# The attention's values of sixteen heads in one unbroken run of matmuls, with six rooms for their operand in a weight slab's place

## The chip, the cores and the metric

The kernel runs on one core of a Trainium2 chip. The metric is the device time of one execution in microseconds (us), the median of several. The core's engines are PE (TensorE: matmuls, and the loads of their stationary operand), DVE (VectorE), ACT (ScalarE), POOL (GpSimd) and SP (SyncE, which here only issues DMAs). Each takes its own instructions strictly in the order of its queue and waits on semaphores for the others. SBUF is the working memory, 128 partitions wide; a size "of SBUF" here is always bytes in each partition. PSUM receives what PE computes.

## The reference

A decoder layer on `x` of 2 x 2048 x 512 and a context of 2 x 77 x 512, in float32: a state-space mixer, then cross attention to the 77 context rows, then a slot-based mixture of 16 experts, each followed by a residual and a LayerNorm. The change touches only the cross attention:

```python
q = (x @ q_w + q_b).reshape(B, T, H, D).transpose(0, 2, 1, 3)      # H = 16 heads of D = 32
k = (context @ k_w + k_b).reshape(B, S, H, D).transpose(0, 2, 1, 3)
v = (context @ v_w + v_b).reshape(B, S, H, D).transpose(0, 2, 1, 3)
att = jnp.einsum('bhtd,bhsd->bhts', q, k) / jnp.sqrt(jnp.float32(D))
att = jax.nn.softmax(jnp.where(causal[None, None, :, :], att, -jnp.inf), axis=-1)
y = jnp.einsum('bhts,bhsd->bhtd', att, v)
return y.transpose(0, 2, 1, 3).reshape(B, T, C) @ o_w + o_b
```

The line that the change rearranges is `y`: 16 products a row block, one for each head, of 77 context rows by 32 features.

## The kernel before

The kernel has four stages on one core. The mixer's scan runs to about 315 us. Then the attention stage goes over 16 tiles of 256 rows (`n` from 0 to 15, `N` = 16), each in two halves `s` of 128 rows; it also holds the mixer's output projection and LayerNorm ahead of the attention, and the dispatch to the slots behind it. Then the sixteen experts stream 192 weight slabs of 1 MB each, and a tail spreads the slots' result back over all rows.

In the attention stage each half tile passes through functions that the code calls by name:

- `load`, `scaled`, `out_proj`, `x1_transposed`, `queries`: the way to the queries, in hi/lo pairs (each product is three matmuls).
- `weigh(n, s, hg)`: scores and softmax of the four heads of group `hg` (0 to 3). DVE, ACT and POOL leave the probabilities in `pp`.
- `gather(n, s, hg)`: four transposes on PE (line 857) turn `pp`, and ACT (groups 0, 1 and 3) or DVE (group 2) copies the result from PSUM to the tile `pt`, 77 partitions by 512 numbers, 2,048 bytes. The pool gives `pt` three rooms (line 854).
- `values(n, s, hg)`: four matmuls, one for each head `r` of the group, with 32 columns of `vt` as the stationary operand. Head `r` writes partitions 32r to 32r + 31 of the PSUM tile `y`, of which there is one. They are in plain float32, and the profile shows two MATMUL records for each, so a group is eight records. After group 3, `y_halves` splits `y` into a hi and a lo tile (ACT, then DVE).
- `o_proj` and the rest: output projection, LayerNorm, the store of `x2` and, from `x2`, the slots' scores and sums (`dispatch`, `p_transposed`, `collect`).

The order of the calls is written out. `PLAN` has eight slots to a tile; in it "W", "G" and "V" stand for `weigh`, `gather` and `values` of the group that is due, with `values` two slots behind `weigh` and `gather` one behind. The lists `head` and `drain` give the first and last calls, and `last` those of the end, where tile 15's work stands in a fixed order on PE. All this sets priorities: the framework then lays out each engine's queue along a modelled timeline, in which an instruction is issued once its operands and its room are ready in the model, those traced earlier first. Two instructions can be tied in order without a wait (`tc.issue_after`, `add_manual_dep`).

The memory matters too. SBUF is two stacks. On the right stand the pools of the attention stage, each below the one that was opened before it: `b_in`, `b_zt`, `b_x1`, `b_sb` (16,736 bytes: maxima, sums, `pp`, the three rooms of `pt`, the halves of `y`), and lowest `b_sb2` (26,880 bytes: the rows `x2`, their halves, `x2T`, the slots' probabilities), which ends at byte 48,960. On the left, above constants and slot sums, stand the slabs A, B, C, ... of 8,192 bytes each for the experts' weights, from byte 15,488 on, over the same bytes that the attention uses from the other side. A slab whose bytes are free can be loaded while the attention runs; the others wait for their rooms. A to D end at 23,680, 31,872, 40,064 and 48,256; E to J follow to 97,408, and the slabs 0 to 9 lie under the right-hand weights. The order in which slabs are filled is written out as well:

```python
'first': 'ABCD06745981I3JK2GHFELM'   # e_Wg of expert 0 in A, B, C, D; its e_W1 in 0, 6, 7, 4; e_W2 in 5, 9, 8, 1; expert 1 from I on
```

Between 6 and 7 come the slots' own weights `d_Wv` and `d_Wo`, in L and M. All slabs are loaded by the SP queue (line 1228).

Of the kernel before, what the change touches and what calls it, by code (L numbers as in the profile page):

```python
# [1 line left out]

# [6 lines left out]
FP = mybir.dt.float32  # L9
# [7 lines left out]
S = 77  # L17
# [220 lines left out]
def tile_decoder(ctx, tc, a, out, dbg=None, upto=9, opt=None):  # L238
    nc = tc.nc
    dbg = dbg or {}  # L240
    opt = opt or TUNED
    pe, act, dve, pool = nc.tensor, nc.scalar, nc.vector, nc.gpsimd

    def mm(o, l, r, start, stop, **kw):
        return pe.matmul(o, lhsT=l, rhs=r, start=start, stop=stop, **kw)  # L245

    def cp(e, o, i):
        (act.copy, dve.tensor_copy, pool.tensor_copy)[e](o, i)  # L248
# [47 lines left out]
    vt = [kv_[b].tile([S, D], FP, name=f"vt{b}") for b in range(B)]  # L296
# [10 lines left out]
    with ExitStack() as st:  # L307
        class Pools:
# [8 lines left out]
            def tile(self, shape, dt, name, tag=None, bufs=1):  # L317
                return self.of[tag or name].tile(shape, dt, tag=tag or name, bufs=bufs, name=name)

        sb = Pools("a_sb", ("xt xh xl raw t1 hi lo dec e0", "BcE CE XE", "XO", "BcO", "CO",  # L320
                            "wtok wdt one chalf offs halo ut xw ssb Bt gm BS CS sw ctxT kst vb qs"), side="right")
# [331 lines left out]
        def chain(*fs):  # L653
            for f in fs:
                yield from f

        def next_weights():

            for j, nm, tags in ((1, "W_outT", ("hi", "lo")), (0, "q_w", ("xh", "xh")), (2, "o_w", ("xl", "xl"))):
                hi, lo = state[nm] = hi_lo_weights("w3", j)  # L660
                for k, tag in zip((0, 2), tags):
                    wr = sb.tile([128, 2, D], FP, tag=tag, bufs=1 + (j != 1), name="wr3")
                    nc.sync.dma_start(wr, rows_of(nm)[:, k:k + 2, :])
                    split(hi[:, k:k + 2], lo[:, k:k + 2], wr, engs[EA.get("wl%d" % j, 2 if j != 1 else 1)], EA.get("wh%d" % j, 0))
                yield
# [18 lines left out]
        for i in range(1, NT - 1):  # L684
            emit(SEQ.get("s%d" % i) or SEQ.get("s") or spread(("S", 16), ("P", 12), ("U", 3), ("V", 2)), "SP",
                 S=chain(scan(2 * i - 1), scan(2 * i)), P=project(i + 1), **later)
        emit(SEQ.get("l") or spread(("S", 16), ("W", 3)) + "S" * 8, "SWUV",
             S=chain(scan(2 * NT - 3), scan(2 * NT - 2), scan(2 * NT - 1)), W=next_weights(), **later)
# [41 lines left out]
    with ExitStack() as st:  # L730
        psb = {tag: st.enter_context(tc.tile_pool(name="b_" + tag, bufs=n, space=PSUM, reuse_waits="tile"))
               for tag, n in (("y", 1), ("mm", 2), ("tr", 2), ("sc", 2))}
        sbq, sb1, sb0 = (st.enter_context(tc.tile_pool(name=nm, bufs=1, side="right", reuse_waits="tile"))
                         for nm in ("b_q", "b_x1T", "b_in"))
        sbz, sbx, sb = (st.enter_context(tc.tile_pool(name=nm, bufs=1, side="right", reuse_waits="tile"))
                        for nm in ("b_zt", "b_x1", "b_sb"))
        sb2 = st.enter_context(tc.tile_pool(name="b_sb2", bufs=1, side="right", reuse_waits="tile"))

        def PT(tag, shape=(128, 512), bufs=2):
            return psb[tag].tile(list(shape), FP, tag=tag, bufs=bufs, name=tag)  # L740
# [14 lines left out]
        N = B * NT  # L755
        ts = [dict() for _ in range(N)]
# [94 lines left out]

        def gather(n, s, hg):
            pp = ts[n].pop(("pp", s, hg))
            pt = sb.tile([S, 4, 128], FP, tag="pt", bufs=opt.get("pt", 3), name="pt")
            tp = PT("tr")
            for r in range(4):
                pe.transpose(tp[0:S, r * 128:r * 128 + 128], pp[:, r, :], ident)  # L857
            cp(EN.get('g%d' % hg, 1 - hg % 2), pt, tp[0:S, :].rearrange("p (r t) -> p r t", t=128))
            ts[n]["pt", s, hg] = pt

        def values(n, s, hg):
            b = n // NT
            if hg == 0:
                ts[n]["y", s] = PT("y", bufs=1)
            yp = ts[n]["y", s]
            pt = ts[n].pop(("pt", s, hg))
            for r in range(4):
                h = hg * 4 + r
                mm(yp[32 * r:32 * r + 32, hg * 128:hg * 128 + 128], vt[b][:, 32 * h:32 * h + 32], pt[:, r, :], True, True)
            if hg == 3 and n < N - 1:  # L870
                y_halves(n, s)

        def y_halves(n, s):
            yh, yl = ts[n]["yv", s] = hi_lo("yv", [128, 4, 128], 1)
            yv = ts[n].pop(("y", s)).rearrange("p (k t) -> p k t", t=128)
            w = 2 if (n, s) == (N - 1, 1) else 4
            for k in range(0, 4, w):
                split(yh[:, k:k + w], yl[:, k:k + w], yv[:, k:k + w])
# [198 lines left out]
        def copy_turned(b, m):  # L1077
# [5 lines left out]
        LV, LG = opt.get("lv", 2), opt.get("lg", 1)  # L1083
        fns = {f.__name__: f for f in (load, scaled, x2_transposed, queries, dispatch, o_proj, p_transposed, out_proj, x1_transposed,
                                       collect, weigh, values, gather, y_halves, o_part, norm, normed, store, halves, x2_high, x2_low,
                                       scores, most, exponentials, sums_so_far, turned_high, turned_low, sums, add_sums, scale, turn_sums,
                                       copy_turned)}
# [103 lines left out]
    sb = cst_.enter_context(tc.tile_pool(name="c_sb", bufs=1, side="left", reuse_waits="tile"))  # L1191
# [3 lines left out]
    if True:  # L1195
# [18 lines left out]
        order, kept = first, {12 * (NE - NL): "0", 12 * NE + 1: "1", 12 * NE + 2: "2"}  # L1214
        while len(order) < 12 * NE + 3:
            n, free = len(order), "6745018923"
# [32 lines left out]
        for q in range(2):  # L1249
            aop = ps.tile([128, 2, B, 64], FP, tag=("mm", "w")[q], bufs=(2, 1)[q], name="aop")  # L1250
            for h in range(2):
                hg = 2 * q + h
# [59 lines left out]
    if True:  # L1312
# [165 lines left out]
        n = said = 0  # L1478
# [77 lines left out]
    with ExitStack() as st:  # L1556
        sb = st.enter_context(tc.tile_pool(name="f_sb", bufs=1, side="right", reuse_waits="tile"))
# [34 lines left out]
        live, at = {}, {}  # L1592
# [196 lines left out]
```

## Time and profile before

| what | value |
|---|---|
| median of three runs | 1490.38 us (1486.42 to 1490.95) |
| the profiled execution | 1492.08 us, its span 1490.2 us |
| mean granted clock of TensorE in it | 0.959 |
| PE busy over the span | 1357.0 us (91%) |
| DVE, ACT, POOL busy | 920.8, 623.2, 451.4 us |
| first and last `y` matmul | 349.8 and 894.9 us |
| first matmul of the experts | 933.4 us |
| last load of a weight slab lands | about 1398 us |
| slab D issued, slab I issued | 330.15 and 899.23 us |

The span is the time from the first to the last instruction; the execution has about 1.9 us around it. The strip in the profile cuts the span into 40 slices of 37.3 us, and each digit is the busy share in tenths. In the PE timeline, matmuls overlap: the next one starts before the modelled end of the one before, so what an instruction costs is the distance between starts. In a line of the timeline, `x8` means eight records in a row. In the list of waits the three numbers are the microseconds in all, the number of times and the longest.

### The profile page before, as it was taken

To read this page: it belongs to the slowest core of one execution; us is meant where nothing else is said; L and a number is where in the kernel's file an instruction comes from. 1 tells how busy PE (TensorE), PEld (TensorE's weight loads), DVE (VectorE), ACT (ScalarE), POOL (GpSimd) and SP (SyncE) were. 2 spreads that over 40 slices of the span, in tenths; PEclk is the share of its full clock that TensorE was granted. 3 is DMA by queue.
4 is the path that set the end of the run, shared out by engine and by line. 5 is a ranking of instruction groups with operands and counts; after the bars stand their busy time and mean duration, and the time that the engine had idled before them with its cause. 6 is when DMAs were issued, how large, how long until landed. Compare 5 with 4: busy or idle time off the path is not lost. (4 is left out here: it accounts for less than half of the span.)

```text
span 1490.2 us, 27755 instructions
## 1 busy us (share of the span) xinstructions
PE 1357.0 (91%) x10442; PEld 985.3 (66%) x10442; DVE 920.8 (62%) x2167; ACT 623.2 (42%) x1694; POOL 451.4 (30%) x498
## 2 busy tenths in 40 slices
PE   7899999978999999999999997978798989988796
PEld 6888878857888888888888786234354444432364
DVE  7997897857888888888888765011111111144397
ACT  5534544525665655665666563110000110034256
POOL 4634543535444444445443321000000000000045
PEclk9999999988999999999999999999998999999899
DMA  9889988894212212322210337999999999999547
GB/s 317 218 189 238 234 211 203 242 260 124 58 58 69 67 58 59 96 59 60 58 44 22 128 136 283 387 417 417 420 418 419 418 419 418 421 420 420 226 157 253
DMA packets 188062, 339.65 MB, mean 228 GB/s; under 512 B 12347, under 2 KB 135739, under 8 KB 163096
## 3 DMA queue, kind: packets, MB, share of 16 engines
q1 hardware_dynamic: 171632, 311.25, 60.3%
q10 hardware_dynamic: 16296, 26.62, 5.2%
q8 instruction: 83, 1.36, 0.4%
q14 instruction: 51, 0.42, 0.1%
HBM read 299.56 MB, written 38.27 MB: 227 GB/s over the span
## 5 line engine op out<-in xcount | busy, mean ns | idle before, releaser
L849 POOL TENSOR_TENSOR pp<-pp,den 128x308 f32<-128x308 f32 x128 | 89.8, 706 | 169.5 <-DVE den L848 65.6
L245 PE MATMUL up<-ew,hT 128*32 128x512 f32 x944 | 125.6, 614 | 10.4 <-DMA ew<-in_e_Wg 7.7
L1354 POOL MEMSET aT<- 128x512 f32 x16 | 8.3, 524 | 385.0 <-PE yac L245 385.0
L1413 DVE TENSOR_TENSOR Qc<-mm,vec 128x512 f32<-128x512 f32 x32 | 22.1, 691 | 149.8 <-PE mm L245 145.5
L245 PEld LDWEIGHTS mm<-xTh,cqh 128*128 128x128 f32 x256 | 50.4, 197 | 70.7 <-issue 42.7
L245 PE MATMUL mm<-xTh,cqh 128*128 128x256 f32 x256 | 81.0, 316 | 14.1 <-ACT xTh L248 14.1
L245 PE MATMUL yac<-ew,aT 128*32 128x512 f32 x488 | 72.7, 692 | 17.3 <-DMA ew<-in_e_W 10.6
L1345 ACT ACTIVATE sv<-up 128x512 f32<-128x512 f32 x32 | 19.1, 598 | 163.5 <-PE up L245 136.9
L248 ACT CAST xTh<-tr 128x512 fp32r<-128x512 f32 x32 | 18.7, 585 | 160.2 <-PE tr L1367 132.6
L857 PE MATMUL tr<-cst,pp 128*77 128x128 f32 x512 | 81.4, 283 | 2.7 <-DVE x1Tl L753 2.2
L248 ACT COPY pt<-tr 77x512 f32<-77x512 f32 x96 | 55.7, 582 | 61.5 <-PE tr L857 33.1
L245 PE MATMUL mm<-x1Th,w30h 128*128 128x256 f32 x256 | 76.4, 299 | 5.1 <-ACT x1Th L752 2.7
L847 ACT ACTIVATE pp<-sc,mx 128x77 f32<-128x77 f32 x240 | 75.3, 326 | 10.7 <-DVE mx L844 10.5
L245 PE MATMUL mm<-xTl,cqh 128*128 128x256 f32 x256 | 75.7, 296 | 2.9 <-DVE xTl L256 2.4
L245 PE MATMUL mm<-x1Tl,w30h 128*128 128x256 f32 x256 | 74.5, 291 | 0.5 <-DVE x1Tl L753 0.5
L245 PE MATMUL mm<-xTh,cql 128*128 128x256 f32 x256 | 74.3, 290 | 0.0
L245 PE MATMUL mm<-x1Th,w30l 128*128 128x256 f32 x256 | 73.9, 289 | 0.0
L857 PEld LDWEIGHTS tr<-cst,pp 128*77 128x77 f32 x512 | 60.1, 149 | 17.8 <-issue 11.4
L256 DVE TENSOR_TENSOR xTl<-tr,xTh 128x512 fp32r<-128x512 f32 x32 | 22.1, 691 | 77.8 <-ACT xTh L248 77.8
L544 DVE SCALAR_TENSOR_TENSOR X<-raw,vec,X 128x256 f32<-128x256 f32 x80 | 66.3, 874 | 5.4 <-ACT X L540 4.9
L775 POOL TENSOR_TENSOR ut<-ut,fb 128x512 f32<-128x512 f32 x32 | 41.4, 1298 | 72.1 <-DMA ut<-Ud 42.1
L248 ACT COPY raw<-pj 128x512 f32<-128x512 f32 x48 | 27.9, 583 | 75.0 <-PE pj L245 49.2
(387 smaller groups left out, 4348.6 us busy)
## 6 DMA issues: line engine op xcount, KB each, us to landing
ew<-in_e_W SPq DMA_DIRECT2D x122, 1024.0 KB, 16.2
ew<-in_e_Wg SPq DMA_DIRECT2D x57, 1024.0 KB, 16.2
BS<-scrBc SPq DMA_DIRECT2D x48, 256.0 KB, 5.1
CS<-scrC SPq DMA_DIRECT2D x48, 256.0 KB, 6.7
xs<-in_xT SPq DMA_DIRECT2D x32, 256.0 KB, 5.6
xt<-in_x SPq DMA_DIRECT2D x32, 256.0 KB, 2.8
ut<-Ud SPq DMA_DIRECT2D x32, 256.0 KB, 3.4
fb<-fd SPq DMA_DIRECT2D x128, 64.0 KB, 3.1
```

Source lines behind the costliest of these rows:

```text
L245: return pe.matmul(o, lhsT=l, rhs=r, start=start, stop=stop, **kw)
L248: (act.copy, dve.tensor_copy, pool.tensor_copy)[e](o, i)
L256: (lo_eng or dve).tensor_tensor(lo, src, hi, ALU.subtract)
L544: dve.scalar_tensor_tensor(dst, raw[:, j, 1 + t:1 + t + TB], w4[:, t:t + 1], dst, ALU.mult, ALU.add)
L775: (act, dve, pool)[EN.get('uf', 1)].tensor_tensor(ut, ut, fb, ALU.mult)
L847: act.activation(pp[:, r, :], sv[:, r, :], AF.Exp, bias=mx[:, h:h + 1], accum_out=den[:, h:h + 1])
L849: (act, dve, pool)[EN.get('d%d' % hg, 2)].tensor_tensor(pp, pp, den[:, h4].unsqueeze(2).to_broadcast([128, 4, S]), ALU.mult)
L857: pe.transpose(tp[0:S, r * 128:r * 128 + 128], pp[:, r, :], ident)
L1345: last["silu"] = act.activation(sv, up, AF.Silu)
L1354: pool.memset(aT, 0.0)
L1413: dve.tensor_tensor(Qc[b][:, mp * 2:mp * 2 + 2, t1:t1 + TB], qq, vec[:, V_CQ + mp * 2:V_CQ + mp * 2 + 2].unsqueeze(2).to_broadcast([128, 2 ...
```

## The change

For tiles 0 to 14, `values` of groups 0, 1 and 2 now does nothing. At group 3 it issues the products of all sixteen heads, group 3 first and then 0, 1 and 2, each matmul tied behind the one before it on PE, and then `y_halves`. Tile 15 keeps its four calls. So `pt` of the first three groups lives until the fourth is there; it gets six rooms instead of three, and a pool of its own, `b_pt`, opened last and so lowest on the right-hand stack. `b_sb` loses the three rooms (6,144 bytes), so that `b_sb2` moves up by as much, and `b_pt` (12,288 bytes) takes bytes 42,816 to 55,104. Slab D ends at 48,256.

```diff
-        sb2 = st.enter_context(tc.tile_pool(name="b_sb2", bufs=1, side="right", reuse_waits="tile"))
+        sb2, sbp = (st.enter_context(tc.tile_pool(name=nm, bufs=1, side="right", reuse_waits="tile")) for nm in ("b_sb2", "b_pt"))
...
-            pt = sb.tile([S, 4, 128], FP, tag="pt", bufs=opt.get("pt", 3), name="pt")
+            pt = sbp.tile([S, 4, 128], FP, tag="pt", bufs=opt.get("pt", 6), name="pt")
...
         def values(n, s, hg):
+
             b = n // NT
-            if hg == 0:
+            one_run = n < N - 1
+            if one_run and hg < 3:
+                return
+            if one_run or hg == 0:
                 ts[n]["y", s] = PT("y", bufs=1)
             yp = ts[n]["y", s]
-            pt = ts[n].pop(("pt", s, hg))
-            for r in range(4):
-                h = hg * 4 + r
-                mm(yp[32 * r:32 * r + 32, hg * 128:hg * 128 + 128], vt[b][:, 32 * h:32 * h + 32], pt[:, r, :], True, True)
-            if hg == 3 and n < N - 1:
+            at = None
+            for g in (3, 0, 1, 2) if one_run else (hg,):
+                pt = ts[n].pop(("pt", s, g))
+                for r in range(4):
+                    h = g * 4 + r
+                    order = tc.issue_after(at.ins) if at is not None else nullcontext()
+                    with order:
+                        at = mm(yp[32 * r:32 * r + 32, g * 128:g * 128 + 128], vt[b][:, 32 * h:32 * h + 32], pt[:, r, :], True, True)
+            if one_run:
                 y_halves(n, s)
```

More of the change, by code (lines that the diff above doesn't have):

```diff
@@ L1 @@
-from contextlib import ExitStack
+from contextlib import ExitStack, nullcontext
 import numpy as np
```

## The prediction

> **What bounds the kernel now.** I read the strip of forty slices first, then the busy times of four stretches that I cut at its breaks, then who waits for whom on PE, then the timelines of PE and of the SP queue. The strip:
>
> ```profile
> PE   7899999978999999999999997978798989988796
> DMA  9889988894212212322210337999999999999547
> ```
>
> In slices 10 to 23 (some 350 to 900 us, the attention) PE is full and DMA is not; from slice 25 on DMA is full. The stretches (columns: length, busy us of PE, PE weight loads, DVE, ACT, POOL, granted clock, DMA share, GB/s):
>
> ```profile
> 405.00:895.00 490.00, 484.21 (x3734) 407.35 (x3732) 396.18 (x1055) 295.04 (x985) 204.04 (x211) 1.00 0.22 69
> 895.00:933.00 38.00, 28.19 (x171) 22.19 (x163) 20.78 (x65) 12.37 (x32) 4.12 (x6) 0.88 0.80 296
> 933.00:1393.00 460.00, 397.71 (x2900) 182.00 (x2904) 91.73 (x173) 70.31 (x112) 8.06 (x16) 0.94 1.01 416
> ```
>
> The attention is bound by PE: 484 of 490 us busy at full clock, and its largest waits there, together about 5.4 us, begin
>
> ```profile
> PE mm L245 <- DVE ql L817: 2.4, 4, 0.6
> PE tr L750 <- DVE dtl L1020: 0.8, 2, 0.4
> PE y L245 <- DVE pt L248: 0.5, 2, 0.3
> ```
>
> The experts (933 to 1393) are bound by the stream of weights at 416 GB/s. That stream can't run far ahead: most slabs lie in rooms that the attention gives up at its end. So what the attention gives, the stream's start and the kernel's end move by, one for one. The 38 us between are a chain of short steps and move as a whole.
>
> What a run of `y` matmuls (the values) costs PE (columns: start, duration, engine, line, what, count; a group of four heads is x8, as each product is two passes):
>
> ```profile
> 602.02 0.39 PE L245 MATMUL mm<-w31l,yyh 128*128 128x512 f32 x1
> 602.24 0.39 PE L245 MATMUL mm<-w31h,yyl 128*128 128x512 f32 x1
> 602.56 0.43 PE L245 MATMUL y<-pt,vt 77*32 77x128 f32 x8
> 602.92 0.66 PE L857 MATMUL tr<-cst,pp 128*77 128x128 f32 x4
> 603.34 0.36 PE L245 MATMUL mm<-x1Th,w30h 128*128 128x256 f32 x1
> ...
> 476.37 0.86 PE L245 MATMUL y<-pt,vt 77*32 77x128 f32 x24
> 477.16 0.39 PE L245 MATMUL mm<-x1Th,w30h 128*128 128x256 f32 x1
> 477.38 0.28 PE L245 MATMUL mm<-x1Tl,w30h 128*128 128x256 f32 x1
> 477.50 0.29 PE L245 MATMUL mm<-x1Th,w30l 128*128 128x256 f32 x1
> ```
>
> Read starts, not durations. A 512-column product normally gives way after 0.23 us (602.02 to 602.24), ahead of `y` after 0.32: 0.09 lost on entry. One group holds PE 0.36 (602.56 to 602.92). What follows is late by 0.06 (four transposes took 0.42; undisturbed ones at 608.63 took 0.36) or by 0.10 (477.16 to 477.38 against 0.12 after it). A run of three groups holds PE 0.79, so each further group in a run adds (0.79 - 0.36) / 2 = 0.215.
>
> **The change, part by part.**
>
> *Runs joined.* A lone group costs 0.09 + 0.36 + 0.06 to 0.10 = 0.51 to 0.55 us, a joined one 0.215. Each run that disappears saves 0.30 to 0.335, say 0.31. The PE timeline from 349 to 895 has 103 `y` runs: 83 of one group, ten of two, eight of three, one group cut in two. The last seven, from 882.04 on, are tile 15's, which keeps its order. The 96 others become 30, one for each half tile of tiles 0 to 14: 66 fewer x 0.31 = **20.5 us** (ends 19.8 and 22.1).
>
> *Runs cut again.* The planner may put a matmul that falls due inside a run. Before, one group of 128 was cut, each having three inner seams: 1 in 384. Thirty runs of 15 seams: 450 / 384 = 1.2 cuts x 0.31 = **+0.4 us**.
>
> *New waits on PE.* With PE 4% shorter the others have less cover. DVE goes from 396/490 (81%) to 396/470 (84%), ACT from 60 to 63%; neither becomes the bound. The order on every queue is fixed beforehand, though, so single waits lengthen. Bounds: none, or all the saving (20 us). I take the nearer row, PE's present 5.4 us of waits, and let half as much again appear: **+3 us**.
>
> *Group 3 first.* The run waits for the newest copy `pt` (ACT, 0.58 us), and behind its first matmul all of PE queues. On the page of before, PE waits 1.1 us in total for `pt` ahead of all 103 runs: there is other work between a group's transposes and its values. The plan puts the gather of group 3 just ahead of the values of group 3, as before, so the same cover serves. 0; if it is gone, rival two.
>
> *Values of groups 0 to 2 later.* Their `pt` are held up to three groups longer, in six rooms instead of three; a half tile holds four and two are left for the next. ACT waited 28.0 us in all for `y` to free a `pt` room (11 times); that mostly ends and is off the path. The two splits of `y` (ACT 0.59, DVE 0.68) start 0.65 us later after group 3; `o_proj` stands two plan slots on, some 8 us. 0.
>
> There a rule of the Trainium skill speaks against the change. ACT's split waits for `y` 23.2 us in 17 cases now, with no PE wait behind it, and the next run that needs the single `y` bank starts some 17 us on. The page TensorEngine Tiling (Array Packing), section Performance Considerations, says that tiling speeds up TensorE but not the emptying of PSUM, which may become the bottleneck. By that rule, as an estimate, each of 30 runs would put 1.27 us of splits on the path, +38 us; by the row, nothing. The sum goes by the row.
>
> *Rooms moved.* By the tile sizes in the code the right-hand stack ended at byte 48,960 and slab D at 48,256. Now `b_sb2` starts 6,144 higher and the six rooms take 42,816 to 55,104, so three of them lie in D. The SP queue of before:
>
> ```profile
> 330.15 0.33 SPq L1228 DMA_DIRECT2D ewD<-in_e_Wg  x1
> ...
> 895.20 0.33 SPq L1228 DMA_DIRECT2D ew<-in_e_W  x1
> 899.23 0.33 SPq L1228 DMA_DIRECT2D ewI<-in_e_W  x1
> ...
> 918.87 0.33 SPq L1228 DMA_DIRECT2D ewG<-in_e_Wg  x1
> 919.29 0.38 SPq L1228 DMA_DIRECT2D ewH<-in_e_Wg  x1
> 919.77 0.38 SPq L1228 DMA_DIRECT2D ewF<-in_e_Wg  x1
> 928.40 0.33 SPq L1228 DMA_DIRECT2D ewE<-in_e_W  x1
> ```
>
> D (1 MB, 2.5 us at 416 GB/s) loses its early load and waits for the last values, about 895. I now lies under the end of `dtl`, whose last product (`mm<-x2h,dtl`) is at 916, and moves from 899 to 916. F comes to lie under the stored `x2` and waits, as E does, for a store that is issued at 921.2. D takes I's place ahead of 3, J, K and 2, which queue behind it; G and H may start with I. The share of DMA by 5 us slices between 895 and 935 leaves 7.6 us idle (most at 910 to 920), so one slab more can vanish. Bounds: -1 us (with F away from the ring the store lands sooner, and E, L and M follow it) and +2.5 us (a whole slab in a full stream). I take **+1**. D's absence at 330, where DMA is full, can help the first loads by up to 2.5 us, but no PE wait there is on D: 0.
>
> *Sum.* -20.5 + 0.4 + 3 + 1 = -16.1 us. The profiled execution took 1492.08 (span 1490.2 and 1.9 around it), so 1476.0 for such a one; the median of the three runs shown is 1490.38, 1.7 lower, and by it 1474.3. I say **1475**. A difference under 0.3% (4.5 us) counts as no change throughout.
>
> **The rivals.**
>
> *One, the gain is handed back.* The other queues' chains, not PE, come to set the pace: two thirds of the 20.5 turn into waits, 1490 - 7 + 1 = 1484, between 1480 and 1490. For it: DVE at 84%, POOL's `pp` waiting on DVE and ACT for over 100 us now. Against: PE waits 5.4 us in 490.
>
> *Two, slower: each run's head waits.* If the planner has nothing to put between the transposes of group 3 and the run, PE stands through transpose, ACT's queue and the 0.58 us copy. At the start of the attention, with nothing else to do, that cost 0.47 us (y at 349.84) and more where ACT was busy; 1.0 for each of 30 runs gives +30 - 20.5 + 1 = +10.5: 1501. It decides from 0.65 us a run. Against: 1.1 us of such waits now.
>
> *Three, D blocks the SP queue.* SP keeps its order. If D is queued where 6, 7, L, M, 4, 5, 9 and 8 go (840 to 892), these eight MB wait until 895: 20 us of transfers into 7.6 us of idle ring, +12.4 - 16: 1486. Against: the queue goes by when rooms come free (slab 7 was issued ahead of L although the code loads it after).
>
> **How the numbers follow.** Likeliest 0.58 (own range 1467 to 1482); rival one 0.18; rival two 0.14; rival three 0.10. Faster: 0.57 + 0.10 of one + 0.03 of three = 0.70; slower: 0.13 of two + 0.04 of three = 0.17; same 0.13. The range 1466 to 1494 leaves out most of rival two and a little below: under 2 in 10.
>
> **What would show it.** Right: some 37 `y` runs, thirty of x32 holding PE about 1.0 us; the stretch from the first `y` to the last some 16 us shorter; D issued near 880 and `hT` ready near 917 instead of 933; the stream's end and the tail behind it unchanged in length. Wrong: PE idle ahead of x32 runs with `pt` as releaser (two), PE waits on DVE and POOL of over 10 us in the attention (one), a hole in the SP queue after 840 (three), or runs cut in many pieces.

## The result, and the profile after

The changed kernel takes 1502.93 us (median of 7 runs, 1499.03 to 1509.06) against 1490.97 us for the kernel before in the same comparison: a ratio of 1.008, 95% interval 1.0058 to 1.0103. It is slower by 0.8%, some 12 us. 1475 was forecast. The profiled execution shown here took 1507.12 us (span 1505.3), 4 us more than the median, and 2.4 us of that lie ahead of the attention (the load of `xt` at 302.5 us in before comes at 304.9), where nothing was changed; differences between the two profiles are read with that in mind.

The stretches of the changed kernel (columns: length, busy us of PE, PE weight loads, DVE, ACT, POOL, granted clock, DMA share, GB/s), cut at its own landmarks, the last `y` matmul at 909.3 and the first matmul of the experts at 948.25:

```profile
405.00:909.40 504.40, 486.00 (x3791) 420.31 (x3789) 396.96 (x1065) 300.34 (x998) 204.16 (x212) 1.00 0.22 67
909.40:948.00 38.60, 28.33 (x171) 22.22 (x163) 21.01 (x66) 12.51 (x32) 4.12 (x6) 0.88 0.83 306
948.00:1408.00 460.00, 398.37 (x2903) 182.50 (x2904) 91.77 (x172) 70.16 (x112) 8.07 (x16) 0.94 1.01 417
```

The attention is 14.4 us longer (490.0 before; up to 2.4 of it is the late start), the steps behind it are 38.6 us (38.0), and the experts stream at 417 GB/s for the same length. So what the change lost it lost in the attention, and stream and tail only moved with its end. The granted clock in each stretch is that of before.

In the attention the runs of `y` came out as meant, where they are whole. From the timelines of PE in the changed kernel (columns: start, duration, engine, line, what, count), a whole run and one that the planner cut:

```profile
436.54 1.08 PE L245 MATMUL y<-pt,vt 77*32 77x128 f32 x32
...
447.03 0.30 PE L245 MATMUL sc<-kbh,ql 128*128 128x308 f32 x1
447.26 1.06 PE L245 MATMUL y<-pt,vt 77*32 77x128 f32 x26
448.25 0.39 PE L245 MATMUL mm<-x1Th,w30h 128*128 128x256 f32 x1
448.47 0.28 PE L245 MATMUL mm<-x1Tl,w30h 128*128 128x256 f32 x1
...
449.67 0.28 PE L245 MATMUL mm<-x1Th,w30l 128*128 128x256 f32 x1
449.88 0.42 PE L245 MATMUL y<-pt,vt 77*32 77x128 f32 x6
450.23 0.50 PE L245 MATMUL mm<-w31h,yyh 128*128 128x512 f32 x1
450.56 0.39 PE L245 MATMUL mm<-w31l,yyh 128*128 128x512 f32 x1
```

PE has 52 runs of `y` where before had 103. Of the thirty that should be whole, 16 are; 14 are in two pieces or more (seven of 26 and 6 records), all of them second halves of a tile, mostly with the twelve query products of the next tile in the gap. What PE waited for between 340 and 930 us in the changed kernel (columns: us in all, times, longest), the four largest rows, all of them ahead of a transpose:

```profile
PE tr L942 <- DVE pt L248: 5.8, 6, 1.0
PE tr L750 <- DVE x L792: 3.1, 1, 3.1
PE tr L857 <- DVE x2Tl L949: 3.0, 3, 1.1
PE tr L750 <- DVE dtl L1028: 2.5, 6, 0.4
```

All rows of this view together are 18.0 us in before and 29.3 us here; in the attention alone, from 405 us to the last `y`, they are 5.7 and 17.8. The slab D, of which the prediction spoke, is issued at 909.42, the moment the values end.

```profile
909.42 0.33 SPq L1236 DMA_DIRECT2D ewD<-in_e_Wg  x1
909.84 4.57 SPq L1236 DMA_DIRECT2D ew<-in_e_W  x2
```

So two things stood to be explained: why 20 us that PE was to save did not come, and why another 12 us were lost.

### The profile page after: what moved, and what is told of

It reads as the page before. It is cut to its first block, busy times and chain, and to the rows that moved or that the text cites. A ratio compares the mean times of both kernels' runs of the same rounds, so it can differ in the third digit from the quotient of the medians.

```text
span 1505.3 us, 27760 instructions
## 1 busy us (share of the span) xinstructions
PE 1353.1 (90%) x10442; PEld 992.3 (66%) x10442; DVE 917.0 (61%) x2167; ACT 624.8 (42%) x1694; POOL 452.5 (30%) x498
## 5 line engine op out<-in xcount | busy, mean ns | idle before, releaser
L857 PE MATMUL tr<-cst,pp 128*77 128x128 f32 x512 | 77.1, 279 | 7.3 <-DVE x2Tl L949 3.0
```

## The experiments

Laying out the queues is the planner's work, and with the change it laid out every queue of the attention anew: up to the first gathers PE's list is that of before, from there on VectorE, ScalarE, GpSimd and PE all stand in another order. To part this from the joining itself, most kernels below tie the queues to a written order. The tie waits for nothing; it only fixes which instruction follows which. The order is a list of positions kept in the kernel, and the diffs show how this list is made from that of before (`t` is the half tile, `d` where its groups stand, `q` the groups in that order, `f` whether an instruction is not of the values; `keep` leaves the groups where they stood, `joined` puts all four where the last stood). The late groups, the halves and the pairs take the groups as they stood, with group 3 last; the other kernels that join all four begin with group 3, as the changed kernel does. In the traces of the kernels "in the old order" the instructions other than the values follow each other on all four engines exactly as in before. Neither before nor the changed kernel was run with nothing but its own order tied, so what the tie alone might cost is not shown; a comparison of two tied kernels does not need it.

Theories one to four were: *one*, the new order loses the time; *two*, the joined run itself does, whatever the order; *three*, the six rooms in a slab's place; *four*, two PSUM rooms for transposes are too few. *Five* and *six* came after the first four runs: *five*, values that come late cost what joining saves; *six*, VectorE is full and PE's savings can't show. Ratios are to the kernel before, with 95% intervals.

**The joined runs in the old order.**

```diff
-                        at = mm(yp[32 * r:32 * r + 32, g * 128:g * 128 + 128], vt[b][:, 32 * h:32 * h + 32], pt[:, r, :], True, True)
+                        at = mm(yp[32 * r:32 * r + 32, g * 128:g * 128 + 128], vt[b][:, 32 * h:32 * h + 32], pt[:, r, :], True, True); YS.setdefault(2 * n + s, []).append(at.ins.name)
...
+        keep_order(tc, ['PE', 'DVE', 'Activation', 'Pool'])
...
+            for i in these:
+                if prev is not None:
+                    tc.add_manual_dep(i, prev.name, mybir.DependencyInfo(
+                        mybir.DependencyClass.NoSync, mybir.DependencyReason.DATA), reason="order")
+                prev = i
```

> The changed kernel, complete, with the queues of TensorE, VectorE, ScalarE and GpSimd tied to the order that they have in the kernel before; each joined run of values stands on TensorE where the last of its four groups stood. SP's queue is left to the planner. Nothing of the computation is left out. Theory one (the change made the planner lay out every queue of the attention anew, and the new order makes TensorE wait at its transposes for rooms that VectorE empties late): those waits go back to the 18 us that the kernel before has between 340 us and the attention's end, few or no runs are cut, and the joined runs bring what the prediction counted, about 15 to 20 us: 1470 to 1476 us, under the kernel before. Theory two (the joined run itself starves VectorE or waits for its last room, whatever the order): 1485 to 1505 us. Theory three (the six rooms in a slab's place cost it): 1495 to 1505 us, like the changed kernel.

Measured: 1491.35 us, 1.0008 (0.9997 to 1.0019). The 12 us of the changed kernel are gone, as theory one said, but the gain of 15 to 20 us is not there: all thirty runs are whole, hold PE 1.01 us, and the kernel takes as long as before. Both theories have half of it. Where the saving went shows in who waits, in the same stretch (405 to 895) of the two kernels. First before:

```profile
ACT pt L248 <- PE tr L857: 30.4, 35, 2.3
ACT pt L248 <- PE y L245: 25.2, 9, 3.1
ACT yvh L248 <- PE y L245: 21.0, 15, 2.5
DVE yvl L256 <- ACT yvh L248: 8.4, 11, 2.4
```

and the joined runs in the old order:

```profile
ACT pt L248 <- PE tr L857: 47.9, 37, 3.0
ACT yvh L248 <- PE y L245: 25.5, 25, 2.9
DVE yvl L256 <- ACT yvh L248: 15.7, 14, 2.9
PE mm L245 <- DVE ql L817: 6.7, 8, 0.9
```

With six rooms ACT no longer waits 25.2 us for `y` to free a room, but it waits 17.5 us longer for the transposes, and DVE stands longer ahead of the split of `y` (8.4 to 15.7). PE's own rows go from 18.0 to 30.2 us (340 to 930); the query products' wait for `ql`, which the prediction showed as 2.4, is 6.7. One such place, in before:

```profile
534.80 0.43 PE L245 MATMUL y<-pt,vt 77*32 77x128 f32 x8
535.15 0.66 PE L857 MATMUL tr<-cst,pp 128*77 128x128 f32 x4
535.57 0.39 PE L245 MATMUL sc<-kbh,qh 128*128 128x308 f32 x1
535.80 0.30 PE L245 MATMUL sc<-kbl,qh 128*128 128x308 f32 x1
535.94 0.28 PE L245 MATMUL mm<-x1Th,w30h 128*128 128x256 f32 x1
```

and with the joined runs (the bracket gives PE's idle time and what ended it):

```profile
531.79 0.60 PE L857 MATMUL tr<-cst,pp 128*77 128x128 f32 x4
532.14 0.39 PE L245 MATMUL sc<-kbh,qh 128*128 128x308 f32 x1
532.37 0.30 PE L245 MATMUL sc<-kbl,qh 128*128 128x308 f32 x1
533.42 0.39 PE L245 MATMUL mm<-x1Th,w30h 128*128 128x256 f32 x1 [0.75 <-DVE ql L817]
```

Before, a group of values stands here (another at 531.56), and the query product goes on without a wait. Joined, both groups stand further on, PE is there sooner, and it waits for VectorE, which takes about as long as before: from the start of `x1Tl` to the end of `ql` 4.7 us, 4.9 before, with one pause of 0.17 us in each. As the other instructions have the same order in both kernels, the distances between their starts on PE can be compared one by one. In the attention, from 340 us on, those next to a run of values shrink by 17.1 us, and all the others grow by 15.2: ahead of query products 7.2, of the transposes of `x` 3.8, of scores 2.6.

**The six rooms alone.**

```diff
-        sb2 = st.enter_context(tc.tile_pool(name="b_sb2", bufs=1, side="right", reuse_waits="tile"))
+        sb2, sbp = (st.enter_context(tc.tile_pool(name=nm, bufs=1, side="right", reuse_waits="tile")) for nm in ("b_sb2", "b_pt"))
...
-            pt = sb.tile([S, 4, 128], FP, tag="pt", bufs=opt.get("pt", 3), name="pt")
+            pt = sbp.tile([S, 4, 128], FP, tag="pt", bufs=opt.get("pt", 6), name="pt")
```

> The kernel before with the six rooms in a pool of their own (and the slabs that move with them) and nothing else: groups of values come one by one as before. Theory one: the planner lays out the queues anew here too, so the time is that of another order, within some 15 us of 1490 us to either side, and where it differs the difference stands in TensorE's waits before transposes, not in the slab stream. Theory three (the rooms cost it): 1500 us or more, as the changed kernel. If neither the order nor the rooms matter: 1488 to 1493 us.

Measured: 1491.53 us, 1.0001 (0.9986 to 1.0016). Neither the rooms nor the slabs that moved cost anything beyond some 2 us either way, and theory three falls. The planner laid out all queues anew here too, without loss: a new order as such need not cost. But it is much nearer to that of before: on PE 296 instructions other than the values have another place in the queue, in the changed kernel 1,543.

**Three rooms for transposes,** in the changed kernel and, as its control, in the kernel before.

```diff
-                for tag, n in (("y", 1), ("mm", 2), ("tr", 2), ("sc", 2))}
+                for tag, n in (("y", 1), ("mm", 2), ("tr", 3), ("sc", 2))}
...
-            return psb[tag].tile(list(shape), FP, tag=tag, bufs=bufs, name=tag)
+            return psb[tag].tile(list(shape), FP, tag=tag, bufs=3 if tag == "tr" else bufs, name=tag)
```

> The changed kernel with three rooms for transposes in PSUM where it has two (the attention uses seven of the eight banks). Theory four (two rooms for transposes are too few once the values come in one run): the waits before transposes, 23 us of the new ones, go, and the time is 1480 to 1488 us. Theory one (what counts is the order that the planner finds, and VectorE's lateness): part of the waits go from the transposes to the next room in the chain, and the time is anywhere from 1485 to 1510 us, another order again.

> The kernel before with three rooms for transposes in PSUM: the control of the run with three rooms. Theory four: the kernel before waits little for these rooms (tens of waits of 0.4 to 1 us, 18 us in all between 340 us and the attention's end), so at most 5 us are gained: 1485 to 1491 us. Theory one: another order, 1480 to 1505 us, and where it is slower the loss stands in TensorE's waits again.

Measured: 1496.77 us, 1.0045 (1.003 to 1.0061), and 1500.21 us, 1.0062 (1.0041 to 1.0083). With a third room the kernel before gets slower by 9 us. Both have yet another order (the first still has 14 of 30 runs in pieces, the control 112 runs of `y` instead of 103), so the two don't price the room by itself. They show that this room is no remedy, and how much a kernel in which nothing is joined can lose by a room and the order that comes with it. For theory four they are inconclusive. (Its 23 us of new waits were too many: the listed waits before transposes are 8.6 us in before and 21.9 in the changed kernel.)

**Late, but not joined.** In the old order, each of groups 0 to 2 ahead of one of the three instructions before group 3:

```diff
+def late(t, d, f):
+    if t >= 30: return keep(t, d, f)
+    q = list(d); spots = []; k = d[q[3]][0] - 1
+    while len(spots) < 3:
+        k -= 1
+        if f(k): spots.append(k)
+    spots = spots[::-1]
+    return [(spots[i], [q[i]]) for i in range(3)] + [(d[q[3]][-1], [q[3]])]
```

> The computation of the kernel before, with every queue in its order but for the values: groups 0 to 2 of a half stand late, each ahead of one of the three instructions that come before group 3, so that they are late but still four short runs with three breaks. Six rooms as in the changed kernel. Theory five (the values of a half that come late cost what joining saves: in the old place they were work for TensorE while VectorE and ScalarE were busy with the softmax; late, TensorE waits there and does them where the others wait for it): 12 to 17 us above the kernel before, 1502 to 1509 us; then joining brings about 15 us and moving costs about 15. Theory six (VectorE is simply full, whatever TensorE does): no change, 1488 to 1494 us.

Measured: 1519.02 us, 1.018 (1.0161 to 1.0198): 27 us slower. The edit does what it says (timeline of PE in this kernel):

```profile
549.33 0.28 PE L245 MATMUL mm<-x2Th,kql 128*128 128x256 f32 x1
549.54 0.43 PE L245 MATMUL y<-pt,vt 77*32 77x128 f32 x8
549.89 0.38 PE L245 MATMUL mm<-x2Th,kqh 128*128 128x256 f32 x1
550.21 0.42 PE L245 MATMUL y<-pt,vt 77*32 77x128 f32 x8
550.56 0.38 PE L245 MATMUL mm<-x2Tl,kqh 128*128 128x256 f32 x1
```

and these are its waits in the stretch of the two lists above:

```profile
ACT pt L248 <- PE tr L857: 48.5, 35, 3.0
ACT yvh L248 <- PE y L245: 42.7, 22, 3.9
DVE yvl L256 <- ACT yvh L248: 24.5, 13, 3.9
```

This is the sum that the prediction lacked. PE has 115 runs here, 12 more than before; at 0.31 us they are 3.7 of the 27 us, so lateness costs some 23. From here to the joined runs in the old order 78 runs go, at 0.31 some 24 us, and the two kernels differ by 1.72%, 25.6 us (22 to 29). So joining pays what was reckoned, and being late costs as much. ACT stands 42.7 us ahead of the split of `y` where it stood 21.0, with everything queued behind it. Start by start on PE, the distances away from the values grow by 18.5 us over before, much as with the joined runs (15.2); those next to the values grow by 9.7, more than the 3.7 reckoned for 12 runs. So 15 to 18 us of the price stand at the other instructions, and the rest lies at the short runs themselves. Theory six falls as it was put: VectorE has the same work, and the time moves by 27 us.

**One half at a time,** in the old order (the run of a half where its last group stood, the other half as before):

```diff
-place = joined
+place = lambda t, d, f: (joined, keep)[t % 2](t, d, f)
```

and with `(keep, joined)` for the other half.

> Every queue in the order of the kernel before; the values of each tile's first half (s = 0, tiles 0 to 14) come in one run where the last of their groups stood, those of the second half stay four short runs in their old places. Theory five, with the chain of instructions of the profiled execution before followed through (each start from the one before it in its queue and from its waits, with that trace's gaps and durations): the first half's run stands where what follows is already late, so that here the move costs more than the joining saves: 4 to 6 us above the kernel before. Theory six: no change. Joining as the prediction priced it: 30 to 45 runs fewer at 0.31 us, 9 to 14 us under.

> As the run before, but the second half's values (s = 1) are joined and the first half's stay as they were. Theory five, followed through in the same way: the second half's run stands ahead of the next queries, where TensorE is ahead of VectorE less often; 4 to 6 us under the kernel before. Theory six: no change. Joining as the prediction priced it: 9 to 14 us under, the same as for the first half.

Measured: 1495.30 us, 1.0015 (1.0001 to 1.0029), with the first half joined, and 1485.46 us, 0.9955 (0.994 to 0.9969), with the second. The signs are as theory five put them, the sizes 2.2 us slower (0 to 4 by the interval; 4 to 6 expected) and 6.7 us faster (5 to 9; 4 to 6 expected). The same edit saves 45 and 22 runs of `y` (58 and 81 are left of 103), and it brings nothing in the half where it saves more. One row of PE's waits tells the halves apart (340 to 930), first half joined:

```profile
PE mm L245 <- DVE ql L817: 7.3, 8, 0.9
```

second half joined:

```profile
PE mm L245 <- DVE ql L817: 3.1, 5, 0.6
```

The first half's run lies on the way to `ql`, the second half's does not. All distances on PE away from the values tell the same: they grow by 18.5 us with the first half joined and by 1.4 with the second. Joining both (1.0008) costs 0.38% or some 6 us (2 to 9) more than the two effects added, so they are not independent.

**Pairs in the first half, one run in the second,** in the old order:

```diff
+def pairs(t, d, f):
+    if t >= 30: return keep(t, d, f)
+    q = list(d); return [(d[q[1]][-1], q[:2]), (d[q[3]][-1], q[2:])]
...
-place = joined
+place = lambda t, d, f: (pairs, joined)[t % 2](t, d, f)
```

> Every queue in the order of the kernel before; the first half's values come as two runs of two groups (one where group 1 stood, one where group 3 stood), the second half's as one run. A candidate to be faster than both kernels. Theory five, followed through in the same way: 5 to 7 us under the kernel before, 1484 to 1487 us. Theory six: no change. Joining as the prediction priced it: 14 to 18 us under.

Measured: 1484.03 us, 0.9939 (0.992 to 0.9958): 9 us faster than before, and by the ratios 21 us faster than the changed kernel. With the second half joined in both, joining the first half's groups in twos makes 9.1 out of 6.7 us, a difference that lies within the intervals; all four in one run had cost 2.2 on their own. The expectations for the two halves and for this kernel were worked out from before's trace: each instruction starts when the one ahead of it in its queue lets it (the gap that the trace shows) and when what it waits for is there. They were 4 to 6 us over before, 4 to 6 under and 5 to 7 under; for the late groups 12 to 17 over were expected. Measured are +2.2, -6.7, -9.1 and +27. The signs and the order hold, the sizes do not.

**The cuts.** The changed kernel in its own order, but for the pieces of 14 runs, which are put together where the last piece stood (`p` are the places of a half's products):

```diff
+        p = [k for k, n in enumerate(names) if yt.get(n) == y]
+        pl[p[-1]] += [-1 - (4 * t + q) for q in (3, 0, 1, 2)]
```

> The changed kernel with TensorE, VectorE, ScalarE and GpSimd tied to its own order, but for one thing: of the 30 runs of values the 14 to 15 that stand in two pieces are put together where the last piece stood. If the cuts cost what they hold TensorE for (some 15 at 0.31 us): 4 to 5 us under the changed kernel, 1496 to 1499 us. If the waits take that back: 1501 to 1504 us, as the changed kernel.

Measured: 1494.10 us, 1.0012 (0.9997 to 1.0027). By the ratios, 0.68% or 10 us of the 12 are the cuts (6 to 14 by the two intervals), 0.7 us each. On PE the place looks like this:

```profile
440.45 0.30 PE L245 MATMUL sc<-kbh,ql 128*128 128x308 f32 x1
440.59 0.28 PE L245 MATMUL mm<-x1Th,w30h 128*128 128x256 f32 x1
...
441.90 0.28 PE L245 MATMUL mm<-x1Th,w30l 128*128 128x256 f32 x1
442.11 1.08 PE L245 MATMUL y<-pt,vt 77*32 77x128 f32 x32
443.12 0.51 PE L245 MATMUL mm<-w31h,yyh 128*128 128x512 f32 x1
443.46 0.40 PE L245 MATMUL mm<-w31l,yyh 128*128 128x512 f32 x1
```

From the score product to the second product of `w31` the cut stretch takes 3.53 us (447.03 to 450.56). Whole, the same instructions take 3.01 (440.45 to 443.46): a cut holds PE 0.52 us longer. Over all 14 places it is 7.5 us. The remaining 2.5 us lie within the interval; what they would be was not shown.

**One side tied at a time.** The ties of the first experiment for PE alone, and for the three other engines without PE:

```diff
-        keep_order(tc, ['PE', 'DVE', 'Activation', 'Pool'])
+        keep_order(tc, ['PE'])
```

> The changed kernel with TensorE alone tied to the order of the kernel before (a joined run where the last group stood); VectorE, ScalarE, GpSimd and SP are laid out by the planner round it. If TensorE's new order is what makes the changed kernel slower than the one with all old orders: 1489 to 1495 us, as with all four tied. If the new order of the other engines does it: 1498 to 1504 us.

> The other side of it: VectorE, ScalarE and GpSimd tied to the order of the kernel before, TensorE left to the planner, with 11 of 30 runs in two pieces. If TensorE's new order is at fault: 1497 to 1504 us. If that of the others: 1489 to 1497 us (the cuts are worth up to 4 us of it).

Measured: 1493.90 us, 1.0009 (0.9994 to 1.0023), and 1504.95 us, 1.0079 (1.0061 to 1.0097). The loss goes with PE's queue. In the second kernel PE is the planner's and has 11 runs in pieces; they alone would be 6 to 8 us of the 12, at 0.52 to 0.7 us each. The rest was not taken apart.

**Left to the planner.** Pairs and one run, without any tie of the queues:

```diff
-            if one_run and hg < 3:
+            if one_run and (hg < 3 if s else hg % 2 == 0):
                 return
-            if one_run or hg == 0:
+            if hg == (3 if one_run and s else 1 if one_run else 0):
...
-            for g in (3, 0, 1, 2) if one_run else (hg,):
+            for g in ((3, 0, 1, 2) if s else (hg, hg - 1)) if one_run else (hg,):
...
-            if one_run:
+            if one_run and hg == 3:
```

> No order is forced: the changed kernel with the first half's values as two runs of two groups and the second half's as one run, all queues laid out by the planner anew. If what a run's place is worth holds through a new layout: 3 to 8 us under the changed kernel by the moves alone. If the layout decides (in the runs so far it gave 0 to 12 us over the order of before): anywhere from 1484 to 1503 us, with the cuts of runs in the layout costing about 0.31 us each.

Measured: 1499.42 us, 1.0047 (1.0031 to 1.0064). By the ratios it is 5 us (1 to 9) under the changed kernel, and 16 us over the same grouping in the old order, with 65 runs of `y` where that has 52. The place of a run seems to be worth something in the planner's layout too, but the cuts come back: 13 more runs are 7 to 9 us at 0.52 to 0.7 us each, and the rest of the 16 was not followed up.

## Why the prediction was wrong

*Runs joined* (-20.5 us) holds. A whole run holds PE 1.01 us as worked out, and 78 runs fewer, from late groups to joined ones, were worth 25.6 us against 24 at 0.31. On PE's timeline the joined runs in the old order save 17.1 us next to the values, a little less than reckoned.

*Values of groups 0 to 2 later* (0) is the step that failed. It saw that the rooms would suffice and that the splits of `y` would start 0.65 us later, and let that cost nothing because `o_proj` stands two plan slots on. It did not ask what PE would do at the places that the values left. The runs put some 23 us in its place with short runs, every other instruction in its old order, and 15.2 us of longer distances on PE with the joined ones, nearly all that joining saved. In the old places a group's values were work that PE had at hand while VectorE made the next operand, as at 534.80; without them it waits there. At the end of the half they stand, all at once, ahead of what the other engines then wait for. How much it costs goes by the place: the first half's run makes the kernel 2.2 us slower, the second half's makes it 6.7 us faster.

The rule of the Trainium skill that was weighed in that step (TensorEngine Tiling (Array Packing), Performance Considerations: emptying PSUM may become the bottleneck) would have given +38 us, and the row that spoke against it, nothing. The measured 23 lie between. But both kernels tile the array alike, and the waits don't show what the rule says: none of PE's rows in the joined kernel is a wait of `y` for its bank. What grew was the wait of the emptying for `y` (21.0 to 42.7 us with late groups), the other way round.

*Runs cut again* (+0.4 us) failed as well. One cut among 384 seams before was taken for a rate, and it is not. A likely reason: before, the planner had places between short runs for whatever fell due, whereas now sixteen products stand in one row where the next tile's queries fall due. 14 of 30 were cut, every one in a second half, and the cuts cost 10 us (6 to 14), the larger part of the 12 by which the kernel is slower. The price of a cut was low too: 0.52 us on PE against 0.31.

*New waits on PE* (+3 us): the 5.4 us that the prediction started from (5.7 by the rows of PE's waits, from 405 us to the last `y`) became 17.8, 12 more and not 3. It gave "all the saving" only as a bound, and in the old order this bound is what happened. These are the waits of the step above, seen from PE, and not a further cost.

*Group 3 first* (0) and *Rooms moved* (+1): in the changed kernel no row of PE's waits has `y` waiting for `pt` (1.3 us before), and the rooms alone gave 1.0001, too coarse to tell 1 us from 0.

Rival one said that two thirds of the gain would be handed back. Its mechanism was right, its size was not: all of it was, and the cuts came on top. Rivals two and three did not occur. With what the runs gave, the sum reads -20.5 + 23 + 10 = +12.5, against 12 measured. That it meets the 12 so closely is in part luck: the last two terms are each uncertain by some 3 or 4 us, and the 23 were measured in the old order.

What stays open: why the waits in the planner's own layout, where they stand before transposes rather than at the split of `y`, come to the same total, and what the 2.5 us of the cuts' 10 are that PE's timeline doesn't show.

## What to carry to other kernels

Work that is moved to a later place to be done cheaper has two prices, and on a busy engine the second is easily missed: in its old place it filled the time in which that engine's next operands were being made. Move it and leave it in pieces, and that price can be measured nearly by itself. And where a planner lays out the queues, an unbroken run exists only if something forbids the break: count the runs after, and price a cut before.

## What was not expected of the hardware

That PE's busy share says little about what PE can give up. Between 405 us and its last `y` PE is busy 484 of 490 us in before. With all thirty runs whole the kernel ends at the same time: over the same stretch PE is busy 472 of 488 us, 12 us less, and idle 10 us more. Not all of the new waiting is in that idle time, as the distances away from the values grow by 14.2 us there: the busy time is reckoned to the modelled ends of overlapping matmuls, and a short wait can lie inside it. Of the prices on PE, entering a run after a 256-column product costs 0.09 us (0.21 against 0.12), and that product then takes 0.32 to the next run instead of 0.12 when it stands alone between two of them (549.89 to 550.21).
